# Half of one stream's convolution on ScalarE and VectorE instead of TensorE, in a selective-scan kernel

## The chip, the cores and the metric

One Trainium2 chip; the kernel runs on one of its cores. The metric is the device time of one execution in microseconds (us). TensorE (PE) multiplies matrices, with PEld for its weight loads; VectorE (DVE), ScalarE (ACT) and GpSimd (POOL) work element by element; SyncE (SP) issues DMAs.

## What is computed

For an input of 4 images, 128 channels, 96 x 96, the reference normalises in groups of 4 channels, reads each image as four sequences of 9216 positions (rows and columns, each forward and backward), runs the function below on each, fuses the four results and adds the input.

```python
def _scan1d(x, ...):
    t = _grouped1x1(x, in_proj_w, in_proj_b, G)          # 4 groups of 32 -> 128 channels
    u, gate = (t[:, :HID], t[:, HID:])                   # HID = 256
    u = jax.nn.silu(u)
    u = lax.conv_general_dilated(u, dw_w, ..., feature_group_count=HID)   # 5 taps a channel
    s = _conv1x1(u, ssm_in_w)                            # 32 channels
    a = DMIN + (DMAX - DMIN) * jax.nn.sigmoid(_conv1x1(u, ssm_delta_w, ssm_delta_b))
    a = jnp.clip(a, 0.0001, 0.9999)
    bb = jnp.tanh(_conv1x1(u, ssm_b_w, ssm_b_b))
    cc = jnp.tanh(_conv1x1(u, ssm_c_w, ssm_c_b))
    prefix = jnp.cumsum(jnp.log(a), axis=-1)
    hst = jnp.exp(prefix) * jnp.cumsum(bb * s * jnp.exp(-prefix), axis=-1)   # h = a*h + bb*s
    u = u + _conv1x1(cc * hst + ssm_d[None, :, None] * s, ssm_out_w)
    u = _grouped1x1(u * jax.nn.sigmoid(gate), mix_w, mix_b, G)
    return _conv1x1(u, out_proj_w, out_proj_b)
```

## The kernel before

Everything is float32. The host lays each sequence out in four phases (position modulo R = 4), so that a tile of 384 columns holds every fourth position of 1536. A phase of the program is one image in one orientation (V for columns, H for rows); it runs two streams s = 0 and 1, the forward and the backward sequence, in six steps of 1536 positions. A step has 8 units: four position phases p times two streams, k = 2p + s. So there are 8 x 6 x 8 = 384 units, and even units belong to stream 0, odd units to stream 1.

The work of a unit t is written out by hand, and each engine runs it in that order (a manual schedule):

- `products` (odd t, for the pair t-3): VectorE multiplies tanh(b) with s out of the PSUM tile pp (L410) and scales s by d (L411) into t1.
- `rows`: TensorE does the in-projection of unit t+8 (pf, L330) and, for the unit bi = t - LAG, the gate's projection (pg) and the recurrence's output projection pz, which reads the buffer t1. ScalarE takes tanh of pg (gv, L348); VectorE adds u to pz (L352) and multiplies by the gate (L353); ScalarE takes silu of pf (sil, L357).
- `conv` for j = 0 and 1, the two halves of 128 channels: eight matmuls each with banded 128 x 32 weights into pc, four 32-column tiles at a time; ScalarE copies pc to u (L375).
- `scan` (unit k = 1, for the step before): one recurrence instruction of 64 x 1536 (L418) over the buffer t0, which starts from the last element of the step before. `outputs` (odd t): c*h (L424), plus d*s (L425), copied to the other partitions by POOL (L426).
- statistics of the next image in even V units (`stats_chunk`), and once an image, in one unit, `stats_finish`: an alternation of small matmuls, VectorE and ScalarE instructions.
- `accumulate` (unit bi-1): the fused output projection py, added into the image-sized buffer acc (L443, L448, L450); in H phases finished rows are stored from acc and the next image's rows are loaded into it.
- `proj`: b, c, delta and s into pp for the pair of units; in odd units the half whose tanh goes to t0 (L396, then two POOL instructions), in even units the half whose tanh goes to t1 (L402).

PSUM: five banks rotate under one tag "x" (pf, pg, pc, py and small ones), one bank is pp's, two are pz's. t0 and t1 have two buffers each, so a step's buffers pass to the step after next. All matmuls go through one helper, line 300. Before the loop the kernel prepares banded weights on POOL and fuses the output weights: products on TensorE, copied out by VectorE (L274, L281), then pb (L286).

Of the kernel before, what the change touches and what calls it, by code (L numbers as in the profile page):

```python
# [30 lines left out]
P = 128  # L34
# [7 lines left out]
R = 4  # L42
# [1 line left out]
NS = HH // LN  # L44
N = LN * WW // R
M = WW // R
LAG = 11
UB = 8


# [1 line left out]
def conv_preact_kernel(  # L52
# [4 lines left out]
    in_wT: bass.AP,  # L57
    in_b: bass.AP,
    dw_v: bass.AP,
    proj_wT: bass.AP,  # L60
    proj_b: bass.AP,
    ssm_d: bass.AP,
# [47 lines left out]
    def psx(name):  # L110
        return ps.tile([P, 512], F32, tag="x", bufs=5, name=name)
# [37 lines left out]
        return stats[b]  # L149

    def stats_finish(b):
        mv = sp.tile([P, 2], F32, tag="mv", name=f"mv_{b}")
        nc.vector.bn_aggr(mv, stats[b].rearrange("p c s -> p (c s)"))
# [7 lines left out]
        nc.vector.scalar_tensor_tensor(ex, dev, dev, mv[:, 1:2], ALU.mult, ALU.add)  # L161
        pv = psx(f"pv_{b}")
# [6 lines left out]
        gm4 = sp.tile([P, 4], F32, tag="gm4", name=f"gm4_{b}")  # L169
        nc.vector.tensor_scalar_mul(gm4, gmask, norm[:, 0:1])  # L170
        pb = psx(f"pbn_{b}")
        nc.tensor.matmul(pb[:, 0:4], wn, gm4, start=True, stop=True)
# [49 lines left out]
    b_in = load(in_b, [P, 4], "b_in")  # L222
    w_proj = load(proj_wT, [P, 2, 4 * MH], "w_proj")
    b_proj = load(proj_b, [P, 2], "b_proj")
    d_sb = load(ssm_d, [P, 1], "d_sb")
# [10 lines left out]
    with tc.tile_pool(name="prep", bufs=1) as pp:  # L236
# [31 lines left out]
        for d in range(4):  # L268
            for j in range(2):
                pt = psx(f"pof_{d}_{j}")  # L270
                nc.tensor.matmul(
                    pt[:, :P], w_out[:, bass.ts(j, P)], w_fuse[:, d, :], start=True, stop=True
                )
                nc.vector.tensor_copy(w_of[:, d, j, :], pt[:, :P])  # L274
        for d in range(4):
            for j in range(2):
                pt = psx(f"pfin_{d}_{j}")
                nc.tensor.matmul(
                    pt[:, :P], w_mix[:, j, :], w_of[:, d, j, :], start=True, stop=True
                )  # L280
                nc.vector.tensor_scalar_mul(w_fin[:, d, j, :], pt[:, :P], 0.5)  # L281
# [16 lines left out]
    def mm(o, col, lhsT, rhs, start, stop):  # L298
        r = slice(32 * col, 32 * col + 32)
        nc.tensor.matmul(o[r, : rhs.shape[-1]], lhsT, rhs, start=start, stop=stop,  # L300
                         skip_group_check=True)


    sils = {}

    def rows(i, bi):

        front = gate = None
        if i is not None:
            step, k = divmod(i, UB)  # L310
            s, g = divmod(k, 4)
            un = units[step * UB + s]
            wn, _, bsil = stats[un["b"]]
# [41 lines left out]
        if front:  # L355
            for j in range(2):
                nc.scalar.activation(  # L357
                    sil[:, j, g, :], pf[j][:, : N + 1], AF.Silu, bias=bsil[:, j, g : g + 1]
                )
            if g == 3:  # L360
                if un["st"] == 0:
                    nc.gpsimd.memset(sil[0:64, :, :, 0:1], 0.0)
                if un["st"] == NS - 1:
                    nc.gpsimd.memset(sil[64:P, :, :, N : N + 1], 0.0)
                load_front(step + 1, s)

    def conv(un, j):
        sil = sils[un["step"], un["s"]]
        if j == 0:
            un["u"] = wk.tile([P, 2, N], F32, tag="u", bufs=LAG + 1, name=f"u_{un['id']}")  # L370
# [4 lines left out]
        nc.scalar.copy(un["u"][:, j, :], pc[:, :N])  # L375

    scans = {}
    qb, qc, qa, qs = (slice(MH * i, MH * (i + 1)) for i in range(4))
# [28 lines left out]
    def products(i):  # L407
        un = units[i]
        (ta, tb), p, pp = scans[un["step"]], un["p"], un["pp"]
        nc.vector.tensor_mul(ta[0:64, p, :], pp[64:P, :N], ta[0:64, p, :])  # L410
        nc.vector.tensor_scalar_mul(tb[64:P, p, :], pp[64:P, :N], d_sb[64:P, :])  # L411

    def scan(step):
        ta = scans[step][0]
        seq = ta.rearrange("p r n -> p (n r)")
        first = units[step * UB]["st"] == 0
        init = 0.0 if first else scans[step - 1][0][0:64, R - 1, N - 1 : N]
        nc.vector.tensor_tensor_scan(  # L418
            seq[0:64], seq[64:P], seq[0:64], init, ALU.mult, ALU.add
        )  # L420

    def outputs(step, p):
# [32 lines left out]
                nc.sync.dma_start(accf[:, r], xr[b + 1, :, r])  # L455


    def unit(t):
        bi = t - LAG
        if t >= 3 and t % 2 and t - 3 < NU:  # L460
            products(t - 3)
        rows(t + UB if t + UB < NU else None, bi if 0 <= bi < NU else None)
        if t < NU:
            conv(units[t], 0)
            conv(units[t], 1)
        if t >= UB + 1 and t % 2 and t - UB - 1 < NU:
            d = units[t - UB - 1]
            if d["p"] == 0:
                scan(d["step"])
            outputs(d["step"], d["p"])  # L470
        if t < NU:
            un = units[t]
            if un["order"] == "V" and t % 2 == 0 and un["b"] + 1 < B:
                stats_chunk(un["b"] + 1, (un["st"] * UB + un["k"]) // 2)
                if un["st"] == NS - 1 and un["k"] == UB - 2:
                    stats_finish(un["b"] + 1)
        if 0 <= bi - 1 < NU:
            accumulate(units[bi - 1])
        if t % 2 and t < NU:
            proj(t - 1, 0)  # L480
        elif t % 2 == 0 and 2 <= t <= NU:
            proj(t - 2, 1)

    stats_finish(b0)
    for i in range(UB):
        rows(i, None)
    with tc.manual_schedule(
        engines={nc.tensor.engine, nc.vector.engine, nc.scalar.engine, nc.gpsimd.engine}
    ):
        for t in range(NU + LAG + 1):  # L490
            unit(t)


_NAMES = [
    "xr", "xs", "in_wT", "in_b", "dw_v", "proj_wT", "proj_b", "ssm_d", "ssm_out_wT",
    "mix_w", "mix_b", "out_w", "out_b", "fuse_wT", "fuse_b",
]

# [61 lines left out]
```

## Time and profile before

| | |
|---|---|
| median of 3 runs | 2842.68 us (2841.59 to 2844.6) |
| the profiled execution | 2841.97 us |
| its span, first to last instruction | 2840.3 us |
| granted TensorE clock, mean | 0.996 of full speed |
| PE / PEld busy | 2749.8 / 1051.9 us |
| DVE / ACT / POOL busy | 1727.9 / 1436.3 / 499.6 us |
| DMA over the span | 134.55 MB, mean 47 GB/s |

A row of a group reads: line, engine, operation, output<-inputs by the program's names, shapes, count | busy us, mean ns of one | idle us of the engine just before them and what ended it. A row of the timeline reads: start in us, length in us, engine, line, operation; in brackets the idle time before it and its releaser. A row of waits reads: who waited <- for whom: us in total, times, longest. TensorE's rows overlap, since four or more small tiles run at once, and float32 matmuls have two records each.

### The profile page before, as it was taken

How to read it: one execution, taken by the hardware profiler on the slowest of the kernel's cores; microseconds unless marked ns; L12 is line 12 of the kernel's file. 1: busy time of each engine (PE TensorE's matmuls, PEld its weight loads, DVE VectorE, ACT ScalarE, POOL GpSimd, SP SyncE). 2: the span in 40 equal slices, each digit the busy share in tenths (PEclk: the TensorE clock that was granted, in tenths of full speed). 3: DMA queues.
4: the chain of work that ended last, by engine and by line, in shares of the span. 5: the costliest groups of instructions: out<-in, count | busy, mean ns of one | idle time of the engine just before them, and what ended most of it. 6: DMA issues, size and time to landing. Idle time of an engine off the chain costs nothing.

```text
span 2840.3 us, 95016 instructions
## 1 busy us (share of the span) xinstructions
PE 2749.8 (97%) x43088; PEld 1051.9 (37%) x43088; DVE 1727.9 (61%) x2119; ACT 1436.3 (51%) x2703; POOL 499.6 (18%) x754
## 2 busy tenths in 40 slices
PE   7999999999999999999999999999999999999998
PEld 3333333333333333333333333333333333333332
DVE  3466655655666666655666666655565656555667
ACT  3555555455555555555555555555555555555542
POOL 4111111111111111111111111111111111111110
PEclk9999999999999999999999999999999999999999
DMA  4111111112321111111232111111123111111111
GB/s 132 43 38 46 41 32 29 25 33 71 91 85 47 39 44 27 33 27 32 76 95 80 41 47 28 33 27 33 27 82 110 26 33 27 33 27 33 27 38 54
DMA packets 79156, 134.55 MB, mean 47 GB/s; under 512 B 11296, under 2 KB 73248, under 8 KB 78752
## 3 DMA queue, kind: packets, MB, share of 16 engines
q1 hardware_dynamic: 76704, 127.64, 16.6%
q8 instruction: 339, 5.55, 0.8%
q10 hardware_dynamic: 2048, 0.83, 0.1%
q14 instruction: 65, 0.53, 0.1%
HBM read 109.55 MB, written 18.87 MB: 45 GB/s over the span
## 4 chain that ended last, share of the span: by engine, by line
PE 82%; DVE 14%; issue 2%; ACT 1%; DMA 1%; SPq 0%; DVEq 0%
PE pc L300 32%; PE pp L300 16%; PE py L300 15%; PE pz L300 9%; PE pf L300 8%; DVE t L418 6%; DVE pz L352 2%; DVE gv L353 2%; PE pg L300 2%; DVE t L424 1%; DVE t L411 1%; ACT t L402 1%; DVE t L425 1%; DVE acc L443 1%; DVE acc L450 0%
## 5 line engine op out<-in xcount | busy, mean ns | idle before, releaser
L300 PE MATMUL pc<-sil,band 128*32 128x384 f32 x12288 | 1072.3, 489 | 50.2 <-DVE acc L443 27.1
L300 PEld LDWEIGHTS pc<-sil,band 128*32 128x32 f32 x12288 | 361.4, 109 | 738.3 <-issue 620.7
L352 DVE TENSOR_TENSOR pz<-pz,u 128x768 f32<-128x768 f32 x384 | 370.5, 965 | 346.4 <-PE pz L300 340.5
L375 ACT COPY u<-pc 128x384 f32<-128x384 f32 x768 | 367.6, 479 | 419.7 <-PE pc L300 415.5
L300 PE MATMUL pp<-u,w_proj 128*32 128x384 f32 x6144 | 571.4, 489 | 0.0
L300 PE MATMUL py<-gv,w_fin 128*32 128x384 f32 x6144 | 570.5, 489 | 0.7 <-DVE gv L353 0.7
L348 ACT ACTIVATE gv<-pg,bnorm 128x384 f32<-128x384 f32 x768 | 403.7, 578 | 101.3 <-PE pg L300 101.3
L300 PE MATMUL pz<-t,w_so 32*32 32x384 f32 x6144 | 430.3, 491 | 6.8 <-DVE gv L353 6.7
L396 ACT ACTIVATE t<-pp,b_proj 128x384 f32<-128x384 f32 x192 | 202.8, 1056 | 424.5 <-PE pp L300 314.5
L357 ACT ACTIVATE sil<-pf,bsilu 128x385 f32<-128x385 f32 x768 | 406.4, 590 | 3.3 <-PE pf L300 3.0
L426 POOL COPY t<-t 64x384 f32<-64x384 f32 x192 | 96.0, 500 | 1754.5 <-DVE t L425 1754.5
L353 DVE SCALAR_TENSOR_TENSOR gv<-gv,pz 128x768 f32<-128x768 f32 x384 | 366.5, 954 | 41.3 <-ACT u L375 0.9
L300 PE MATMUL pf<-x_in,wn 32*32 32x385 f32 x6144 | 356.7, 503 | 0.0
L300 PE MATMUL pg<-x_in,wn 32*32 32x384 f32 x6144 | 356.3, 494 | 0.0
L410 DVE TENSOR_TENSOR t<-pp,t 64x384 f32<-64x384 f32 x192 | 169.9, 885 | 298.8 <-ACT t L402 298.7
L402 ACT ACTIVATE t<-pp,b_proj 64x384 f32<-64x384 f32 x192 | 110.6, 576 | 409.0 <-PE pp L300 409.0
L300 PEld LDWEIGHTS pp<-u,w_proj 128*32 128x32 f32 x6144 | 204.5, 110 | 295.5 <-issue 267.3
L300 PEld LDWEIGHTS py<-gv,w_fin 128*32 128x32 f32 x6144 | 200.8, 110 | 298.2 <-issue 223.7
L399 POOL TENSOR_SCALAR t<-t 64x384 f32<-64x384 f32 x192 | 181.7, 946 | 317.4 <-ACT t L396 313.6
L300 PEld LDWEIGHTS pz<-t,w_so 32*32 32x32 f32 x6144 | 168.6, 103 | 163.1 <-issue 93.1
L443 DVE TENSOR_TENSOR acc<-py,acc 128x384 f32<-128x384 f32 x192 | 107.0, 557 | 194.0 <-PE py L300 176.4
L400 POOL TENSOR_SCALAR t<-t 64x384 f32<-64x384 f32 x192 | 182.6, 951 | 15.9
(60 smaller groups left out, 1006.3 us busy)
## 6 DMA issues: line engine op xcount, KB each, us to landing
x_in<-in_xs SPq DMA_DIRECT2D x96, 385.0 KB, 4.3
x_in<-in_xs SPq DMA_DIRECT2D x384, 96.2 KB, 2.4
out<-acc SPq DMA_DIRECT2D x24, 768.0 KB, 4.0
xs<-in_xr SPq DMA_DIRECT2D x72, 192.0 KB, 2.3
acc<-in_xr SPq DMA_DIRECT2D x18, 768.0 KB, 4.8
acc<-in_xr SPq DMA_DIRECT2D x24, 192.0 KB, 3.8
w_fuse<-in_fuse_wT ACTq DMA_DIRECT2D x1, 256.0 KB, 3.8
w_proj<-in_proj_wT ACTq DMA_DIRECT2D x1, 128.0 KB, 4.5
```

The lines of the kernel that those rows point to most:

```text
L300: nc.tensor.matmul(o[r, : rhs.shape[-1]], lhsT, rhs, start=start, stop=stop, skip_group_check=True)
L348: nc.scalar.activation(gv[:, j, :], pg[j][:, :N], AF.Tanh, bias=gbn[:, 2 + j : 3 + j], scale=0.5)
L352: nc.vector.tensor_add(pz[:, :, :N], pz[:, :, :N], bu["u"])
L353: nc.vector.scalar_tensor_tensor(gv, gv, 1.0, pz[:, :, :N], ALU.add, ALU.mult)
L357: nc.scalar.activation(sil[:, j, g, :], pf[j][:, : N + 1], AF.Silu, bias=bsil[:, j, g : g + 1])
L375: nc.scalar.copy(un["u"][:, j, :], pc[:, :N])
L396: nc.scalar.activation(ta[:, p, :], pp[:, :N], AF.Tanh, bias=b_proj[:, 0:1])
L399: nc.gpsimd.tensor_scalar(a, a, half, DMIN + half, ALU.mult, ALU.add)
L400: nc.gpsimd.tensor_scalar(a, a, 0.9999, 0.0001, ALU.min, ALU.max)
L402: nc.scalar.activation(tb[0:64, p, :], pp[0:64, :N], AF.Tanh, bias=b_proj[0:64, 1:2])
L410: nc.vector.tensor_mul(ta[0:64, p, :], pp[64:P, :N], ta[0:64, p, :])
L418: nc.vector.tensor_tensor_scan(seq[0:64], seq[64:P], seq[0:64], init, ALU.mult, ALU.add)
```

## The change

Stream 0's second half of channels (j = 1, even units) is no longer convolved on TensorE. Its silu tile is laid out with all 128 channels on the partitions for each position phase; one ScalarE instruction scales it by tap 0 into a PSUM bank, in the unit before (`taps(un, [0])`), and four VectorE instructions add taps 1 to 4 in place, the last one into u, at the start of the unit. A tap's weight is a per-partition scalar from a new small input, w_tap. d*s moves from VectorE to ScalarE (`skip`). The recurrence is two instructions of 768 positions, in the units k = 1 and 2, after the accumulate. `outputs` come two units later, and LAG is 12. `stats_finish` is a generator that advances by one part a unit. The copies of the fused weights are ScalarE's.

```diff
-LAG = 11
+LAG = 12
@@ stats_finish
         nc.vector.bn_aggr(mv, stats[b].rearrange("p c s -> p (c s)"))
+        yield
...
-                nc.vector.tensor_copy(w_of[:, d, j, :], pt[:, :P])
+                nc.scalar.copy(w_of[:, d, j, :], pt[:, :P])
...
-                nc.vector.tensor_scalar_mul(w_fin[:, d, j, :], pt[:, :P], 0.5)
+                nc.scalar.mul(w_fin[:, d, j, :], pt[:, :P], 0.5)
@@ rows
-                    mm(pf[j], c, wn[r, 32 * g : 32 * g + 32], x_in[s][r, c, :], True, True)
+                    m, q = (c, g) if by_taps(s, j) else (g, c)
+                    mm(pf[j], c, wn[r, 32 * m : 32 * m + 32], x_in[s][r, q, :], True, True)
@@ new
+    def by_taps(s, j):
+        return s == 0 and j == 1
+    def taps(un, ks):
+        sil, j = sils[un["step"], un["s"]], 1
+        if 0 in ks:
+            un["pt"] = psx(f"pt_{un['id']}")
+        for k in ks:
+            off, q = divmod(un["p"] + k, R)
+            src, part = sil[:, j, q, off : off + N], un["pt"][:, :N]
+            if k == 0:
+                nc.scalar.activation(part, src, AF.Copy, scale=w_tap[:, 0:1])
+            else:
+                nc.vector.scalar_tensor_tensor(
+                    un["u"][:, j, :] if k == K - 1 else part,
+                    src, w_tap[:, k : k + 1], part, ALU.mult, ALU.add)
@@ products, skip, scan
-        nc.vector.tensor_scalar_mul(tb[64:P, p, :], pp[64:P, :N], d_sb[64:P, :])
+    def skip(i):
+        nc.scalar.activation(
+            tb[64:P, un["p"], :], un["pp"][64:P, :N], AF.Copy, scale=d_sb[64:P, :])
+    def scan(step, part):
+        r = bass.ts(part, R * N // 2)
+        if part:
+            init = ta[0:64, R - 1, N // 2 - 1 : N // 2]
@@ unit, new order
+        bi, k = t - LAG, t % UB
+        if t % 2 and 0 <= t - 3 < NU:
             products(t - 3)
+        if t % 2 and 0 <= t - 11 < NU:
+            outputs(d["step"], d["p"])          # d = units[t - 11]
+        if un and k % 2 == 0:
+            taps(un, range(1, K))
         rows(t + UB if t + UB < NU else None, bi if 0 <= bi < NU else None)
+        if t % 2 and 0 <= t - 3 < NU:
+            skip(t - 3)
+        if un:
+            conv(un, 0)
+            if k % 2:
+                conv(un, 1)
         if 0 <= bi - 1 < NU:
             accumulate(units[bi - 1])
+        if later:
+            next(later[0], None)
...                                             # statistics chunk
+        if k in (1, 2) and 0 <= t // UB - 1 < NU // UB:
+            scan(t // UB - 1, k - 1)
+        if t + 1 < NU:
+            new_u(units[t + 1])
+            if k % 2:
+                taps(units[t + 1], [0])
...                                             # proj as before
```

More of the change, by code (lines that the diff above doesn't have):

```diff
@@ L59, in conv_preact_kernel @@
     dw_v: bass.AP,
+    dw_c: bass.AP,
     proj_wT: bass.AP,
@@ L161, in stats_finish @@
         nc.vector.scalar_tensor_tensor(ex, dev, dev, mv[:, 1:2], ALU.mult, ALU.add)
+        gm4 = sp.tile([P, 4], F32, tag="gm4", name=f"gm4_{b}")
+        nc.vector.tensor_scalar_mul(gm4, gmask, norm[:, 0:1])
+        yield
         pv = psx(f"pv_{b}")
@@ L222, in conv_preact_kernel @@
     b_in = load(in_b, [P, 4], "b_in")
+    w_tap = load(dw_c, [P, K], "w_tap")
     w_proj = load(proj_wT, [P, 2, 4 * MH], "w_proj")
@@ L357, in rows @@
                 nc.scalar.activation(
-                    sil[:, j, g, :], pf[j][:, : N + 1], AF.Silu, bias=bsil[:, j, g : g + 1]
+                    sil[:, j, g, :],
+                    pf[j][:, : N + 1],
+                    AF.Silu,
+                    bias=bn[:, j : j + 1] if by_taps(s, j) else bsil[:, j, g : g + 1],
                 )
             if g == 3:
[L361 to L364, printed above, removed]
+                for j in range(2):
+                    if un["st"] == 0:
+                        r = (slice(0, P), slice(0, 2)) if by_taps(s, j) else (slice(0, 64), slice(0, 4))
+                        nc.gpsimd.memset(sil[r[0], j, r[1], 0:1], 0.0)
+                    if un["st"] == NS - 1:
+                        r = (slice(0, P), slice(2, 4)) if by_taps(s, j) else (slice(64, P), slice(0, 4))
+                        nc.gpsimd.memset(sil[r[0], j, r[1], N : N + 1], 0.0)
                 load_front(step + 1, s)
@@ L375, in conv, with new_u @@
         nc.scalar.copy(un["u"][:, j, :], pc[:, :N])
+    def new_u(un):
+        un["u"] = wk.tile([P, 2, N], F32, tag="u", bufs=LAG + 1, name=f"u_{un['id']}")
+    def taps(un, ks):
[10 more added lines that the diff above has]
+                    un["u"][:, j, :] if k == K - 1 else part,
+                    src,
+                    w_tap[:, k : k + 1],
+                    part,
+                    ALU.mult,
+                    ALU.add,
+                )
     scans = {}
@@ L410, in products @@
         nc.vector.tensor_mul(ta[0:64, p, :], pp[64:P, :N], ta[0:64, p, :])
-        nc.vector.tensor_scalar_mul(tb[64:P, p, :], pp[64:P, :N], d_sb[64:P, :])
-    def scan(step):
+    def skip(i):
+        un = units[i]
+        tb = scans[un["step"]][1]
+        nc.scalar.activation(
+            tb[64:P, un["p"], :], un["pp"][64:P, :N], AF.Copy, scale=d_sb[64:P, :]
+        )
+    def scan(step, part):
         ta = scans[step][0]
         seq = ta.rearrange("p r n -> p (n r)")
-        first = units[step * UB]["st"] == 0
-        init = 0.0 if first else scans[step - 1][0][0:64, R - 1, N - 1 : N]
+        r = bass.ts(part, R * N // 2)
+        if part:
+            init = ta[0:64, R - 1, N // 2 - 1 : N // 2]
+        elif units[step * UB]["st"] == 0:
+            init = 0.0
+        else:
+            init = scans[step - 1][0][0:64, R - 1, N - 1 : N]
         nc.vector.tensor_tensor_scan(
-            seq[0:64], seq[64:P], seq[0:64], init, ALU.mult, ALU.add
+            seq[0:64, r], seq[64:P, r], seq[0:64, r], init, ALU.mult, ALU.add
         )
@@ L455, in accumulate @@
                 nc.sync.dma_start(accf[:, r], xr[b + 1, :, r])
+    later = []
     def unit(t):
-        bi = t - LAG
-        if t >= 3 and t % 2 and t - 3 < NU:
+        bi, k = t - LAG, t % UB
+        un = units[t] if t < NU else None
+        if t % 2 and 0 <= t - 3 < NU:
             products(t - 3)
-        rows(t + UB if t + UB < NU else None, bi if 0 <= bi < NU else None)
[L463 to L476, printed above, removed]
+        if t % 2 and 0 <= t - 11 < NU:
+            d = units[t - 11]
+            outputs(d["step"], d["p"])
+        if un and k % 2 == 0:
+            taps(un, range(1, K))
+        rows(t + UB if t + UB < NU else None, bi if 0 <= bi < NU else None)
+        if t % 2 and 0 <= t - 3 < NU:
[4 more added lines that the diff above has]
+                conv(un, 1)
         if 0 <= bi - 1 < NU:
             accumulate(units[bi - 1])
-        if t % 2 and t < NU:
+        if later:
+            next(later[0], None)
+        if un and un["order"] == "V" and k % 2 == 0 and un["b"] + 1 < B:
+            stats_chunk(un["b"] + 1, (un["st"] * UB + k) // 2)
+            if un["st"] == NS - 1 and k == UB - 2:
+                later[:] = [stats_finish(un["b"] + 1)]
+        if k in (1, 2) and 0 <= t // UB - 1 < NU // UB:
[4 more added lines that the diff above has]
+                taps(units[t + 1], [0])
+        if k % 2 and un:
             proj(t - 1, 0)
-        elif t % 2 == 0 and 2 <= t <= NU:
+        elif k % 2 == 0 and 2 <= t <= NU:
             proj(t - 2, 1)
-    stats_finish(b0)
+    for _ in stats_finish(b0):
+        pass
     for i in range(UB):
         rows(i, None)
+    new_u(units[0])
+    taps(units[0], [0])
     with tc.manual_schedule(
@@ L525 @@
         .reshape(P, 2, 4, 8),
+        "dw_c": v["dw_w"].reshape(HID, K)[P:],
         "proj_wT": halves(
```

9 lines of the change are left out of this document (3 added, 6 removed).

## The prediction, made before the changed kernel was run

> **What bounds the kernel now.** I read the page first: the shares of the engines and the chain that ended last.
>
> ```profile
> PE 2749.8 (97%) x43088; PEld 1051.9 (37%) x43088; DVE 1727.9 (61%) x2119; ACT 1436.3 (51%) x2703; POOL 499.6 (18%) x754
> PE 82%; DVE 14%; issue 2%; ACT 1%; DMA 1%; SPq 0%; DVEq 0%
> PE pc L300 32%; PE pp L300 16%; PE py L300 15%; PE pz L300 9%; PE pf L300 8%; DVE t L418 6%; DVE pz L352 2%; DVE gv L353 2%; PE pg L300 2%; DVE t L424 1%; DVE t L411 1%; ACT t L402 1%; DVE t L425 1%; DVE acc L443 1%; DVE acc L450 0%
> ```
>
> TensorE (PE) works without a break and the convolution (pc) is the largest part of the chain. The timeline shows two consecutive units of the middle, an odd one with the recurrence and the even one behind it:
>
> ```profile
> 999.63 1.47 PE L300 MATMUL py<-gv,w_fin 128*32 128x384 f32 x16
> 1001.17 0.56 DVE L443 TENSOR_TENSOR acc<-py,acc 128x384 f32<-128x384 f32 x1 [0.18 <-PE py L300]
> 1002.32 0.51 PE L300 MATMUL pf<-x_in,wn 32*32 32x385 f32 x2
> ...
> 1010.01 1.12 PE L300 MATMUL pz<-t,w_so 32*32 32x384 f32 x16
> 1011.06 2.79 PE L300 MATMUL pc<-sil,band 128*32 128x384 f32 x32
> 1013.67 1.47 PE L300 MATMUL py<-gv,w_fin 128*32 128x384 f32 x16
> 1013.72 3.41 DVE L418 TENSOR_TENSOR_SCAN t<-t,t 64x1536 f32<-64x1536 f32 x1
> 1014.96 1.48 PE L300 MATMUL pp<-u,w_proj 128*32 128x384 f32 x16
> 1016.36 0.51 PE L300 MATMUL pf<-x_in,wn 32*32 32x385 f32 x2
> 1017.04 1.11 PE L300 MATMUL pz<-t,w_so 32*32 32x384 f32 x16
> 1017.16 0.89 DVE L424 TENSOR_TENSOR t<-t,t 64x384 f32<-64x384 f32 x1
> 1017.22 0.97 ACT L396 ACTIVATE t<-pp,b_proj 128x384 f32<-128x384 f32 x1 [2.83 <-DVE t L418]
> 1018.08 0.56 DVE L425 TENSOR_TENSOR t<-t 64x384 f32<-64x384 f32 x1
> 1018.67 0.56 DVE L443 TENSOR_TENSOR acc<-py,acc 128x384 f32<-128x384 f32 x1
> 1019.28 2.79 PE L300 MATMUL pc<-sil,band 128*32 128x384 f32 x32 [1.13 <-DVE acc L443]
> ```
>
> Counting from a unit's first pf: pz at 0.68, pc at 1.72 (1011.06 is 1.05 behind pz), py 2.61 after pc, the next unit at 7.02 (1002.32 + 2 x 7.02 = 1016.36). The accumulate of the last py ends at 1001.73, 0.59 before the next pf. Once a step (8 units) the recurrence holds the accumulate back, and pc waits 1.13 for the bank that it frees:
>
> ```profile
> L300 PE MATMUL pc<-sil,band 128*32 128x384 f32 x12288 | 1072.3, 489 | 50.2 <-DVE acc L443 27.1 <-DVE acc L450 23.0
> ACT t L396 <- DVE t L418: 109.9, 39, 3.0
> ```
>
> 50.2 us in all are these waits. So the bank that pc takes is the accumulate's, freed just ahead of the rows' own. The second row: the first tanh of a step waits for the recurrence, which only reads one element of the buffer that the tanh takes over. A buffer is passed on only when all that read its old content are done.
>
> **The change, part by part.** Prices:
>
> ```profile
> L353 DVE SCALAR_TENSOR_TENSOR gv<-gv,pz 128x768 f32<-128x768 f32 x384 | 366.5, 954 | 41.3 <-ACT u L375 0.9 <-DVE pz L352 0.9
> L352 DVE TENSOR_TENSOR pz<-pz,u 128x768 f32<-128x768 f32 x384 | 370.5, 965 | 346.4 <-PE pz L300 340.5
> L375 ACT COPY u<-pc 128x384 f32<-128x384 f32 x768 | 367.6, 479 | 419.7 <-PE pc L300 415.5 <-ACT sil L357 0.2
> L396 ACT ACTIVATE t<-pp,b_proj 128x384 f32<-128x384 f32 x192 | 202.8, 1056 | 424.5 <-PE pp L300 314.5 <-DVE t L418 109.9
> L402 ACT ACTIVATE t<-pp,b_proj 64x384 f32<-64x384 f32 x192 | 110.6, 576 | 409.0 <-PE pp L300 409.0
> L410 DVE TENSOR_TENSOR t<-pp,t 64x384 f32<-64x384 f32 x192 | 169.9, 885 | 298.8 <-ACT t L402 298.7
> L418 DVE TENSOR_TENSOR_SCAN t<-t,t 64x1536 f32<-64x1536 f32 x40 | 136.4, 3409 | 1.3
> L411 DVE TENSOR_SCALAR t<-pp,d_sb 64x384 f32<-64x384 f32 x192 | 119.8, 624 | 2.8
> L443 DVE TENSOR_TENSOR acc<-py,acc 128x384 f32<-128x384 f32 x192 | 107.0, 557 | 194.0 <-PE py L300 176.4 <-PE pg L300 8.2 <-PE pz L300 4.7
> L448 DVE SCALAR_TENSOR_TENSOR acc<-py,b_fin,acc 128x384 f32<-128x384 f32 x96 | 59.3, 618 | 179.1 <-PE py L300 179.1
> ```
>
> (1) TensorE loses pc for j=1 in every even unit: two of four rounds, 2.61/2 = 1.305 us, 192 times: -250.6. An even unit becomes 5.71, a pair 12.73.
>
> (2) In its place ScalarE writes tap 0 into a PSUM bank (nearest L402, 0.58, without the 0.479 copy of L375) and VectorE adds four taps. A tap is L448's form (pointer scalar, one PSUM input), 0.618; PSUM as output adds L352 less L353, 0.01. Four with three gaps of 0.03 (as between L424 and L425 in the timeline): T = 2.59. VectorE's sum: 1727.9 + 768 x 0.624 - 119.8 (L411, moved to ScalarE, 0.58 each) + 10 (two halves of the recurrence at 1.81 for one of 3.41: 3.2 of it is elements, 0.2 fixed, my split) = 2097. ScalarE: 1436 + 192 x (0.58 + 0.58 - 0.48) = 1567. Neither is the bound by its sum; it is the order that costs.
>
> (3) The tap bank. The taps are VectorE's first work in an even unit and free their bank ahead of the rows', so pc takes it, as it took the accumulate's. An ordinary pair: accumulate done at -0.59, taps from -0.56 to 2.03, pc at 2.08 instead of 1.72: 0.36 of wait, a new one in units 0, 4 and 6 of each step. [...]
>
> (4) The recurrence. Its first half stands in unit 1 behind the accumulate, and so ahead of the taps of unit 2: taps done at 3.87, pc at 3.92, wait 2.20. Should pc take the first gate bank instead: the tanh L396 waits for that half (to 1.25), then 1.06, then the first gv (L402's kind, 0.58): pc at 2.9, wait 1.2. No row decides between them; I take the middle, 1.70. The second half (1.84 with its gap) stands behind the accumulate of unit 2 and reaches 1.3 to 1.9 into unit 3.
>
> (5) LAG 12. The last pz that reads a step's buffer t1 moves from unit 2 to unit 3, while the tanh L402 that takes this buffer over stays at the end of unit 2. By the L396 row it waits for all readers: until pz of unit 3 is done (0.68 + 1.11), to 2.41 with its own 0.58, not 0.71. The products (L410) start at 2.44; products 0.92, outputs 1.50, pz and gv 2.01, accumulate 0.56, no gap left: about 7.4, 0.35 to 0.43 into unit 4 instead of 0.59 ahead of it. Taps to 2.97, pc at 3.02: wait 1.30 in unit 4 in place of 0.36. The products wait behind that tanh, and skip (ScalarE) behind the products, but skip's slot, near 4.6, is long before pp of unit 3.
>
> Sum of waits in a step: 0.36 + 1.70 + 1.30 + 0.36 = 3.72; 46.5 full steps: +173. The old 50.2 go. In the first 12 units there is no gate work: tap 0 comes at the end of the odd unit as before, but pc sooner, by pz's 1.05 at least: T has less cover, an estimated 1.6 more in five pairs, +8.
>
> (6) Statistics over units:
>
> ```profile
> 1046.32 1.11 PE L300 MATMUL pz<-t,w_so 32*32 32x384 f32 x16
> 1053.55 0.36 PE L172 MATMUL pbn<-gm,wn 128*128 128x4 f32 x2 [1.10 <-DVE gm L170]
> 1058.92 1.12 PE L300 MATMUL pz<-t,w_so 32*32 32x384 f32 x16
> ```
>
> 12.60 instead of 7.02, three times; three small matmuls of 0.36 stay each time: -(5.58 - 1.1) x 3 = -13.4. The rest hides in units with waits.
>
> (7) Weight copies on ScalarE:
>
> ```profile
> 24.71 2.31 DVE L281 TENSOR_SCALAR w_fin<-pfin 128x128 f32<-128x128 f32 x8
> 29.75 1.84 PE L286 MATMUL pb<-b_out,w_fuse 128*128 128x1 f32 x8
> 31.71 0.79 DVE L153 BATCH_NORM_AGGREGATE mv<-bn 128x2 f32<-128x144 f32 x1
> ```
>
> The statistics' matmul queues behind pb, and pb behind copies that wait among VectorE's bn_stats. ScalarE is free there; at best the 4.7 between 27.0 and 31.7 go, at worst nothing: -4.
>
> (8) Image change, three times. The first V accumulate waits for the store and reload of acc:
>
> ```profile
> 801.08 0.56 DVE L450 TENSOR_TENSOR acc<-py,acc 128x384 f32<-128x384 f32 x1
> 801.66 0.35 SPq L453 DMA_DIRECT2D out<-acc  x1
> 805.87 0.33 SPq L455 DMA_DIRECT2D acc<-in_xr  x1
> 810.39 0.56 DVE L443 TENSOR_TENSOR acc<-py,acc 128x384 f32<-128x384 f32 x1 [3.84 <-PE pg L300]
> ```
>
> 8.7 us pass. The shift by a unit makes the two accumulates 6.5 apart, and taps stand behind: +2 each, +6. SP's order of loads and stores is otherwise the same. LAG's extra unit at the end costs VectorE's 0.97 + 0.95 + 0.56 and half of L424 and L425, 3.2, less 2.3 of gate work (pz 1.05, py 1.29) that leaves the loop: +0.9. The more and smaller memsets on POOL (18% busy) and the load of w_tap lie beside other work: nothing; without cover some 0.1 each.
>
> Sum: -250.6 - 50.2 + 173 + 8 - 13.4 - 4 + 6 + 0.9 = -130.3, from the profiled execution's 2841.97 (span 2840.3; 0.7 under the median of the runs, 2842.68): **2712 us**.
>
> **Rivals.** (A) No late tanh: the buffer is passed on by parts, since the slices differ. The L396 row speaks against it. 0.94 x 46.5 less: 2668. (B) pc takes a bank other than the taps', in all pairs (a gate bank, free at about pc's turn in ordinary pairs). Left are 1.2 in unit 2 and 0.4 in unit 4 (the rows' own wait for the late accumulate), 74 for 173, and the 8 fall away: 2605. For it: nothing says the pool must keep its order with a new tenant. (C) Cheap taps, at L443's 0.557 and without gaps: T 2.23, the two waits of 0.36 go and the others lose as much, about 1.2 a step: 2656. L448's 0.618 for the very form speaks against it. [...] (D) Dear taps, which makes it slower: every 0.1 us on a tap adds 0.4 to all four waits of a step, 75 us in all; from 0.80 a tap the gain is gone. L410 pays 0.885 for 384 elements beside PSUM, on strided data; at that price, 0.26 more than mine, it would be 2712 + 195 = 2907. The taps read contiguous rows, so little speaks for it. (E) The freed TensorE time comes back nearly whole in waits of several kinds, within 0.2%.
>
> **How the numbers follow.** Forecast 0.37, A 0.18, B 0.20, C 0.08, D 0.08, E 0.04; 0.05 for A and B or C together, under 2595. Range 2595 to 2775: its low end takes in B, its high end a tap chain with gaps of 0.09 and the 2.20 of point 4 (2712 + 33 + 23, and some for the bounds of 5 and 7). Unlisted waits can push toward slower. About 0.2% is what a measurement of this kernel can tell from no change: faster 0.88, same 0.03, slower 0.09.
>
> **What would show it.** pc with 9216 records; a group of 768 VectorE taps near 0.62 us; pc's idle row naming the taps with some 0.4 in ordinary pairs and 1 to 2 in unit 2; L402's successor waiting for a pz in unit 3 once a step; VectorE near 78%; no 5.6 us hole at the statistics. It is wrong if pc's idle falls to some tens of us (B), if taps take 0.8 (D), or if TensorE waits elsewhere, on sil or gv.

## The result, and the profile after

The changed kernel takes 2751.27 us (median of 4 runs, 2736.34 to 2756.05) against 2843.07 us for the kernel before in the same session: a ratio of 0.9667, interval [0.9636, 0.9699], 92 us less. The profiled execution is the one of 2736.34 us, with a span of 2734.7 us. The page's rows of the engines and of the chain:

```profile
PE 2546.5 (93%) x40016; PEld 961.4 (35%) x40016; DVE 2054.6 (75%) x2727; ACT 1565.1 (57%) x2912; POOL 496.1 (18%) x786
PE 64%; DVE 30%; ACT 2%; DMA 2%; issue 1%; ACTq 0%; DVEq 0%; SPq 0%
PE pc L308 25%; PE py L308 16%; DVE pt L406 12%; PE pp L308 10%; PE pz L308 6%; PE pf L308 6%; DVE u L406 4%; DVE t L468 3%; DVE gv L365 2%; DVE acc L498 2%; DVE pz L364 2%; DVE acc L493 2%; DVE t L448 1%; DVE t L474 1%; PE pg L308 1%
```

TensorE is no longer busy without a break (93% of the span, 97% before), and the taps (L406), absent before, are 16% of the chain. The groups, with shapes kept apart:

```profile
L308 PE MATMUL pc<-sil,band 128*32 128x384 f32 x9216 | 833.3, 494 | 153.2 <-DVE u L406 145.9 <-ACT gv L360 7.3
L406 DVE SCALAR_TENSOR_TENSOR pt<-sil,w_tap,pt 128x384 f32<-128x384 f32 x576 | 357.3, 620 | 43.6 <-ACT pt L404 28.5
L406 DVE SCALAR_TENSOR_TENSOR u<-sil,w_tap,pt 128x384 f32<-128x384 f32 x192 | 118.1, 615 | 6.8
```

The convolution has lost 239 us of busy time (1072.3 before) and 3072 records; 153.2 us of idle time stand ahead of it in place of 50.2, nearly all ended by the last tap. The waits of the tanh that fills the recurrence's second tile:

```profile
ACT t L440 <- PE pp L308: 300.6, 146, 2.6
ACT t L440 <- PE pz L308: 194.9, 46, 5.5
```

46 times, once a step, it waits for pz instead of for its own input. The timeline of units 0, 1 and 2 of one step:

```profile
617.60 1.48 PE L308 MATMUL pp<-u,w_proj 128*32 128x384 f32 x16
618.39 1.93 DVE L406 SCALAR_TENSOR_TENSOR pt<-sil,w_tap,pt 128x384 f32<-128x384 f32 x3
619.68 1.12 PE L308 MATMUL pz<-t,w_so 32*32 32x384 f32 x16
620.35 0.61 DVE L406 SCALAR_TENSOR_TENSOR u<-sil,w_tap,pt 128x384 f32<-128x384 f32 x1
621.02 1.50 PE L308 MATMUL pc<-sil,band 128*32 128x384 f32 x16 [0.23 <-DVE u L406]
...
626.75 2.79 PE L308 MATMUL pc<-sil,band 128*32 128x384 f32 x32
...
631.55 1.81 DVE L468 TENSOR_TENSOR_SCAN t<-t,t 64x768 f32<-64x768 f32 x1
632.72 1.12 PE L308 MATMUL pz<-t,w_so 32*32 32x384 f32 x16
633.39 1.94 DVE L406 SCALAR_TENSOR_TENSOR pt<-sil,w_tap,pt 128x384 f32<-128x384 f32 x3
635.36 0.61 DVE L406 SCALAR_TENSOR_TENSOR u<-sil,w_tap,pt 128x384 f32<-128x384 f32 x1
636.03 1.72 PE L308 MATMUL pc<-sil,band 128*32 128x384 f32 x16 [2.19 <-DVE u L406]
637.50 2.81 PE L308 MATMUL py<-gv,w_fin 128*32 128x384 f32 x16
```

In unit 0 pc starts 1.34 us after pz, and 0.05 us after the last tap has ended. In unit 1, which has no taps, it starts 1.04 after pz; in unit 2 half a recurrence (L468) runs before the taps and pc starts 3.31 after pz. Right behind that gap py takes 2.81 us, not the 1.47 that it took before. The same place in windows of 2 us (the third number from the end of a row is the granted TensorE clock):

```profile
634.00:636.00 2.00, 0.00 (x0) 0.00 (x0) 1.89 (x5) 2.00 (x5) 1.45 (x2) 1.00 0.24 58
636.00:638.00 2.00, 1.97 (x20) 0.77 (x24) 1.81 (x2) 0.35 (x2) 0.34 (x1) 0.80 0.00 0
638.00:640.00 2.00, 2.00 (x16) 0.65 (x12) 0.00 (x0) 0.28 (x1) 0.00 (x0) 0.50 0.00 0
640.00:642.00 2.00, 2.00 (x36) 0.73 (x44) 1.61 (x2) 0.00 (x0) 0.00 (x0) 0.85 0.00 0
```

The clocks read 1.00, 0.80, 0.50 and 0.85. A window of 2 us loses 2 us times what its clock lacks: 0.4 + 1.0 + 0.3 = 1.7 us, as much as 3.4 us at half clock would lose. A step (8 units) is best read from the same pc of consecutive steps (here the first four records of unit 0), in the timelines of before and of after:

```profile
545.41 0.53 PE L300 MATMUL pc<-sil,band 128*32 128x384 f32 x4
602.74 0.53 PE L300 MATMUL pc<-sil,band 128*32 128x384 f32 x4
```

```profile
399.38 0.53 PE L308 MATMUL pc<-sil,band 128*32 128x384 f32 x4 [0.17 <-DVE u L406]
455.94 0.53 PE L308 MATMUL pc<-sil,band 128*32 128x384 f32 x4 [0.23 <-DVE u L406]
...
510.96 0.53 PE L308 MATMUL pc<-sil,band 128*32 128x384 f32 x4 [0.23 <-DVE u L406]
565.99 0.53 PE L308 MATMUL pc<-sil,band 128*32 128x384 f32 x4 [0.23 <-DVE u L406]
```

57.33 us before; 55.03 after in a step whose clock stays up, 56.56 in one with a half-clock stretch.

### The profile page after: what moved, and what is told of

It reads as the page before. It is cut to its first block, busy times and chain, and to the rows that moved or that the text cites. A ratio compares the mean times of both kernels' runs of the same rounds, so it can differ in the third digit from the quotient of the medians.

```text
span 2734.7 us, 89086 instructions
## 1 busy us (share of the span) xinstructions
PE 2546.5 (93%) x40016; PEld 961.4 (35%) x40016; DVE 2054.6 (75%) x2727; ACT 1565.1 (57%) x2912; POOL 496.1 (18%) x786
## 3 DMA queue, kind: packets, MB, share of 16 engines
q1 hardware_dynamic: 76704, 127.64, 17.5%
## 4 chain that ended last, share of the span: by engine, by line
PE 64%; DVE 30%; ACT 2%; DMA 2%; issue 1%; ACTq 0%; DVEq 0%; SPq 0%
PE pc L308 25%; PE py L308 16%; DVE pt L406 12%; PE pp L308 10%; PE pz L308 6%; PE pf L308 6%; DVE u L406 4%; DVE t L468 3%; DVE gv L365 2%; DVE acc L498 2%; DVE pz L364 2%; DVE acc L493 2%; DVE t L448 1%; DVE t L474 1%; PE pg L308 1%
## 5 line engine op out<-in xcount | busy, mean ns | idle before, releaser
L308 PE MATMUL pc<-sil,band 128*32 128x384 f32 x9216 | 833.3, 494 | 153.2 <-DVE u L406 145.9
L308 PE MATMUL py<-gv,w_fin 128*32 128x384 f32 x6144 | 584.5, 499 | 0.7 <-DVE gv L365 0.7
L308 PEld LDWEIGHTS pc<-sil,band 128*32 128x32 f32 x9216 | 258.7, 109 | 709.2 <-issue 272.2
L308 PE MATMUL pz<-t,w_so 32*32 32x384 f32 x6144 | 445.9, 492 | 4.6 <-DVE gv L365 4.5
L391 ACT COPY u<-pc 128x384 f32<-128x384 f32 x576 | 271.6, 480 | 231.8 <-PE pc L308 227.0
L440 ACT ACTIVATE t<-pp,b_proj 64x384 f32<-64x384 f32 x192 | 110.7, 577 | 495.5 <-PE pp L308 300.6
L406 DVE SCALAR_TENSOR_TENSOR pt<-sil,w_tap,pt 128x384 f32<-128x384 f32 x576 | 357.3, 620 | 43.6 <-ACT pt L404 28.5
L308 PE MATMUL pg<-x_in,wn 32*32 32x384 f32 x6144 | 375.6, 494 | 4.2 <-DVE acc L493 4.2
L308 PE MATMUL pf<-x_in,wn 32*32 32x385 f32 x6144 | 375.9, 503 | 0.0
L434 ACT ACTIVATE t<-pp,b_proj 128x384 f32<-128x384 f32 x192 | 198.8, 1036 | 285.4 <-PE pp L308 187.1
L448 DVE TENSOR_TENSOR t<-pp,t 64x384 f32<-64x384 f32 x192 | 171.4, 893 | 221.4 <-ACT t L440 221.4
L437 POOL TENSOR_SCALAR t<-t 64x384 f32<-64x384 f32 x192 | 174.3, 908 | 876.1 <-ACT t L434 876.1
L369 ACT ACTIVATE sil<-pf,bsilu 128x385 f32<-128x385 f32 x576 | 314.9, 586 | 3.2 <-PE pf L308 3.0
```

The lines of the kernel that those rows point to most:

```text
L369: nc.scalar.activation(sil[:, j, g, :], pf[j][:, : N + 1], AF.Silu, bias=bn[:, j : j + 1] if by_taps(s, j) else bsil[:, j, g : g + 1],)
L406: nc.vector.scalar_tensor_tensor(un["u"][:, j, :] if k == K - 1 else part, src, w_tap[:, k : k + 1], part, ALU.mult, ALU.add,)
L434: nc.scalar.activation(ta[:, p, :], pp[:, :N], AF.Tanh, bias=b_proj[:, 0:1])
L437: nc.gpsimd.tensor_scalar(a, a, half, DMIN + half, ALU.mult, ALU.add)
L440: nc.scalar.activation(tb[0:64, p, :], pp[0:64, :N], AF.Tanh, bias=b_proj[0:64, 1:2])
```

## The experiments

Theory: the time that left TensorE is real, and what came back is three waits, each with its own cause (the bank that the taps hold, the half recurrence ahead of the taps of unit 2, the tanh held up by its buffer), and the half clock after the longest of them. The rivals were that pc would be as late in another bank, that the taps are late by themselves, and that the buffer doesn't matter.

**Where the taps' sum lies.** With a bank of its own (so four rotate):

```diff
-        return ps.tile([P, 512], F32, tag="x", bufs=5, name=name)
+        return ps.tile([P, 512], F32, tag="x", bufs=4, name=name)
-            un["pt"] = psx(f"pt_{un['id']}")
+            un["pt"] = ps.tile([P, 512], F32, tag="t", name=f"pt_{un['id']}")
```

> The tap sum gets a PSUM bank of its own and the rotating pool has four banks instead of five. Theory (the wait is for the bank that the taps free): pc in even units takes a gate bank that is free in time; the idle time ahead of pc falls from 153 us to about 60, what is left being some 1.2 in unit 2 (the tanh that waits for the recurrence holds the gate's own tanh) and under 1 in unit 4; with no gap of 2 us TensorE's clock keeps 1.0 in the loop; 2625 to 2670 us against 2751. Rival (VectorE is simply too late in even units, whatever the bank, or four banks are too few): the wait moves to the accumulate's bank or to the rows, and the time stays at 2735 to 2760 or rises.

2655.08 us, ratio to the kernel before 0.9344 [0.933, 0.9358]: the time is as expected, though pc's idle time fell to 94 us and not to 60. pc's group, then units 2 and 3 with the tanh (ACT) that stands ahead of the gate's own:

```profile
L308 PE MATMUL pc<-sil,band 128*32 128x384 f32 x9216 | 830.9, 493 | 94.3 <-ACT gv L360 93.6
```

```profile
622.21 0.94 ACT L434 ACTIVATE t<-pp,b_proj 128x384 f32<-128x384 f32 x1 [2.76 <-DVE t L468]
623.54 1.50 PE L308 MATMUL pc<-sil,band 128*32 128x384 f32 x16 [0.94 <-ACT gv L360]
...
629.44 0.57 ACT L440 ACTIVATE t<-pp,b_proj 64x384 f32<-64x384 f32 x1 [3.85 <-PE pz L308]
630.53 2.79 PE L308 MATMUL pc<-sil,band 128*32 128x384 f32 x32 [1.19 <-ACT gv L360]
```

No wait names the taps any more. What is left are gate banks, freed late by ScalarE: in unit 2 its tanh (L434) waits for the half recurrence, in unit 3 the other tanh (L440) waits for pz.

With the sum in SBUF and five rotating banks kept:

```diff
-            un["pt"] = psx(f"pt_{un['id']}")
+            un["pt"] = wk.tile([P, N], F32, tag="pt", bufs=1, name=f"pt_{un['id']}")
```

> The changed kernel with one edit: the taps' sum lies in an SBUF tile, not in one of the five rotating PSUM banks. Theory (what costs 2.2 us in unit 2 and 0.3 us in units 0, 4 and 6 is the bank that the taps hold, not that they are late as such): the convolution finds a free bank, its idle time behind the taps goes, the late tanh stays; 2640 to 2670 us as with a bank of its own. Rival (taps are slower in SBUF, 0.7 us or more each, so that VectorE becomes the bound): 2720 to 2850 us, with TensorE waiting for VectorE's accumulate in every even unit.

2572.98 us, 0.9047 [0.9033, 0.9061]: better than either expected, although the taps became dearer, as the rival said. The instructions of the taps' line (min/median/max ns), with the sum in a bank of its own and then in SBUF:

```profile
L406 DVE SCALAR_TENSOR_TENSOR u<-sil,w_tap,pt x192: 614/615/617, 40.5 to 2592.4; 128x384 f32<-128x384 f32 x192
```

```profile
L406 DVE SCALAR_TENSOR_TENSOR u<-sil,w_tap,pt x192: 617/1176/1410, 40.9 to 2507.8; 128x384 f32<-128x384 f32 x192
```

and the last tap of units 2 and 4 in the second, with GpSimd's work:

```profile
602.72 1.14 POOL L438 TENSOR_SCALAR t<-t 64x384 f32<-64x384 f32 x1
603.07 1.20 DVE L406 SCALAR_TENSOR_TENSOR u<-sil,w_tap,pt 128x384 f32<-128x384 f32 x1
...
614.84 1.14 POOL L438 TENSOR_SCALAR t<-t 64x384 f32<-64x384 f32 x1
616.42 0.62 DVE L406 SCALAR_TENSOR_TENSOR u<-sil,w_tap,pt 128x384 f32<-128x384 f32 x1
```

Beside this GpSimd instruction the last tap takes 1.20, without one 0.62. Of the run's 768 taps 269 take over 0.7 us, and each of them overlaps a GpSimd instruction; the 385 that overlap none take 0.62 at most. (The other 114 overlap one too and are no slower.) The kernel is still faster: VectorE, 86% busy, has room, and pc, 11.2 us idle in all, stands behind a late bank only in three places, with the accumulate.

Is it the fifth rotating bank, then? The sum in SBUF again, but with `bufs=4` for tag "x", so that one bank is left empty:

> The changed kernel with the taps' sum in SBUF and four rotating PSUM banks in place of five (one bank is left empty). Theory (the 80 us by which the sum in SBUF beat a bank of its own is the fifth rotating bank: with four, the convolution and gate banks come late in units 2 and 3): 2645 to 2680 us, TensorE waiting in front of the convolution for ScalarE's gate as with the bank of its own. Rival (the 80 us come from the sum's place itself, though a tap costs more there): within 10 us of the sum in SBUF with five banks, 2565 to 2585 us.

2701.72 us, 0.9506 [0.9492, 0.952]. Taking away the one bank costs 129 us, so the rival falls. It is also 47 us more than with a bank of its own, where four banks rotate too, and pc's idle time behind ScalarE is the same in both (93.9 and 93.6 us). The difference lies ahead of pc, in unit 3:

```profile
582.14 0.55 DVE L500 TENSOR_TENSOR acc<-py,acc 128x384 f32<-128x384 f32 x1
582.74 0.10 PEld L308 LDWEIGHTS pg<-x_in,wn 32*32 32x32 f32 x1 [0.70 <-DVE acc L500]
585.67 2.79 PE L308 MATMUL pc<-sil,band 128*32 128x384 f32 x32 [1.19 <-ACT gv L360]
```

VectorE, behind the dearer taps of unit 2, does the accumulate late, and pg waits for the bank that it frees: from the unit's first pf to the last pg 1.26 us pass instead of 0.46, some 38 us over the run. So the dear taps do cost where banks are short.

**The late tanh.** Three buffers for the tile that it fills:

```diff
-                wk.tile([P, R, N], F32, tag="t1", name=f"t1_{step}"),
+                wk.tile([P, R, N], F32, tag="t1", bufs=3, name=f"t1_{step}"),
```

> The buffer t1 exists three times instead of twice, nothing else. Theory (a buffer is passed on only when all its readers are done, so the tanh of unit 2 waits for pz of unit 3): the 195 us of that tanh's waits for pz vanish, products start some 1.7 us earlier in unit 3, pc's wait in unit 4 falls from about 1.2 to 0.3; about 40 us less, 2700 to 2720. Rival (unit 4 is late because the second half of the recurrence reaches into unit 3): the waits for pz vanish but unit 4 stays late, 2740 to 2755.

2708.41 us, 0.9523 [0.9503, 0.9543]: 43 us from one buffer. The waits now:

```profile
ACT t L440 <- PE pp L308: 407.2, 192, 3.5
```

All 192 wait for their input, none for pz. Unit 4 starts pc 1.34 after pz (median), like units 0 and 6; unit 2 stays at 3.31.

Both edits together, with three buffers for t0 as well:

> Own bank for the tap sum, and t0 and t1 three times each. Theory: besides what the two changes alone give, the tanh of unit 1 no longer waits for the recurrence, so the gate bank is free in time in unit 2 too; left is VectorE's lateness after two recurrence halves in a row, under 1 us in unit 4; no half clock in the loop: 2550 to 2600. Rival (TensorE cannot use its freed time since VectorE with its 2055 us of work and fixed order is the real bound): above 2640, with new waits for the accumulate or gv.

2580.9 us, 0.9084 [0.9071, 0.9098]: the time is as expected. pc's idle time is 2.5 us in all (in unit 3 the rows ahead of it still take 0.5 longer, since pg waits for the accumulate's bank):

```profile
L308 PE MATMUL pc<-sil,band 128*32 128x384 f32 x9216 | 829.8, 492 | 2.5 <-ACT gv L360 1.5
```

The three buffers added to the sum in SBUF:

> The changed kernel with the taps' sum in SBUF, five rotating PSUM banks, and three buffers for each of the recurrence's two tiles. Theory (the late tanh still holds ScalarE back once a step; what TensorE still waits, 40 us over the whole run, is partly VectorE late behind it): the wait of ScalarE's tanh for the gate's products goes, 2535 to 2565 us. Rival (five free banks already cover the late tanh, and what is left is VectorE, slowed by taps that share SBUF with GpSimd): the same within 6 us, 2567 to 2580 us.

2572.71 us, 0.9054 [0.904, 0.9067]; without them it was 0.9047 [0.9033, 0.9061]. The tanh's wait for pz (170.4 us and 46 times with two buffers) is gone, yet the time stays: the rival was right, five free banks cover the late tanh.

**The recurrence and the taps.** The whole recurrence in unit 1, as before the change, but the rest changed:

```diff
-        r = bass.ts(part, R * N // 2)
+        r = slice(0, R * N)
-        if k in (1, 2) and 0 <= t // UB - 1 < NU // UB:
+        if k == 1 and 0 <= t // UB - 1 < NU // UB:
```

> The recurrence in one instruction again, at the place of its first half. Theory: taps of unit 2 start 1.6 us later (3.41 for 1.81), pc's wait there grows from 2.2 to 3.8, 74 us; the longer gap lets TensorE's clock fall to half more often than in 18 of 48 steps, up to 50 us more: 2825 to 2880, and a mean clock under 0.975. Rival (the clock has nothing to do with the gap): the clock stays at 0.98 and the time at 2820 to 2830.

2790.79 us, 0.9821 [0.9785, 0.9857]: slower by 40 us than in halves, less than either expected. pc waited 2.6 in unit 2, not 3.8, for it then stood behind another bank, and not at all in the second step of each phase. From pz to pc the waits add up to 187 us over the run, as with halves (185); what got worse is the clock (78.4 us lost in the loop for 29.0, counted as in the last section):

```profile
L308 PE MATMUL pc<-sil,band 128*32 128x384 f32 x9216 | 852.5, 503 | 154.9 <-ACT gv L360 100.0 <-DVE u L406 54.9
```

Which half delays which unit? With three buffers for both tiles (`bufs=3` for t0 and t1, not shown), the halves after units 1 and 3:

```diff
-LAG = 12
+LAG = 14
-        if t % 2 and 0 <= t - 11 < NU:
-            d = units[t - 11]
+        if t % 2 and 0 <= t - 13 < NU:
+            d = units[t - 13]
-        if k in (1, 2) and 0 <= t // UB - 1 < NU // UB:
-            scan(t // UB - 1, k - 1)
+        if k in (1, 3) and 0 <= t // UB - 1 < NU // UB:
+            scan(t // UB - 1, k // 2)
```

> The version with three buffers for the recurrence's tiles (2708 us; taps still in a rotating bank), with the recurrence's halves in units 1 and 3 rather than 1 and 2 and the outputs two units later. Theory (prediction's step 4: the 2.2 us in unit 2 come from the half of the recurrence that stands ahead of that unit's taps on VectorE, and the half clock follows that gap): the wait of unit 2 falls to the 0.3 us of the other even units, 47 times 1.9 us and some 20 halvings at 1.7 us less, 2585 to 2625 us. Rival (the taps of unit 2 are late whatever runs ahead of them, or the half in unit 3 delays an accumulate as much): 2660 to 2720 us.

2858.58 us, 1.0056 [1.0039, 1.0073]: slower than before the change. The expectation had the place wrong. `scan` stands at the end of a unit, so a half in an odd unit is ahead of the next even unit's taps, and this run has two such places a step, where the changed kernel has one (its second half, in unit 2, precedes unit 3, which has no taps). It doubled the suspected cost:

```profile
603.63 1.50 PE L308 MATMUL pc<-sil,band 128*32 128x384 f32 x16 [2.19 <-DVE u L406]
618.64 2.53 PE L308 MATMUL pc<-sil,band 128*32 128x384 f32 x16 [2.19 <-DVE u L406]
...
633.38 1.50 PE L308 MATMUL pc<-sil,band 128*32 128x384 f32 x16 [0.22 <-DVE u L406]
646.42 1.50 PE L308 MATMUL pc<-sil,band 128*32 128x384 f32 x16 [0.23 <-DVE u L406]
```

Against the version with three buffers for t1 it is 150 us more: from pz to pc 81 us more over the run (227 for 146), and 68 more lost to the clock in the loop (105.5 for 37.4).

The converse, halves after units 2 and 4 (`k in (2, 4)`, `k // 2 - 1`), so that no taps follow either:

> As the version with the recurrence's halves after units 1 and 3 (2859 us, two waits of 2.2 us a step), but with the halves after units 2 and 4, so that each stands ahead of an odd unit, in which VectorE has no taps. Theory (prediction's step 4, the half ahead of the taps is the wait): every even unit waits only the 0.3 us of the others; against the version with three buffers (2708 us, one such wait a step) 47 times 1.9 us and most of its 53 us of lost clock fall away, 2560 to 2610 us, with a clock of 0.99. Rival (a half after unit 4 makes the accumulate of unit 5 late, as the halves after units 1 and 3 did with a bank of its own): 2620 to 2700 us.

2598.12 us, 0.9135 [0.912, 0.9151]: from the same edits as the run above, and 260 us apart from it by the place of two instructions. The rival falls. pc's group:

```profile
L308 PE MATMUL pc<-sil,band 128*32 128x384 f32 x9216 | 827.8, 491 | 44.8 <-DVE u L406 44.8
```

Only the 0.3 of each even unit is left, and the clock is 0.997.

The halves after units 1 and 3 on the version with a bank of its own and three buffers (the diff of LAG above):

> The own-bank, three-buffer version with the recurrence's halves in units 1 and 3 rather than 1 and 2, and the outputs two units later. Theory (the 0.5 us that TensorE still waits in unit 3 of each step comes from VectorE being behind after two halves of 1.8 us in a row): up to 20 us less, 2557 to 2575 us. Rival (each half now delays an accumulate by itself, in units 3 and 5, and the fill grows by two units): the same or more, 2580 to 2605 us.

2603.57 us, 0.9158 [0.9144, 0.9171]: 23 us slower than without it, the rival's case. pc comes 0.5 us late in two units a step where there was one (pz to pc 1.6 us for 1.05 to 1.12), since pg waits for the accumulate's bank, 20 us over the run; the two more units at the end take 6.

**Statistics and start**, both on that version. Finishing the statistics in one unit (`for _ in stats_finish(...): pass`):

> The own-bank, three-buffer version with the finishing of the batch statistics back in one unit. Theory (the prediction's statistics term: a hole of 5.6 us at each of the three finishes that the trace of before shows, of which spread finishing leaves about 1.1, and the half clock that followed each hole there): three times 4.5 us, about 13 us more, 2590 to 2600 us, with a hole of 4 to 6 us on TensorE at each finish. Rival (the finish lies beside TensorE's work now that two of four convolution rounds have left it): the same time within 4 us, 2577 to 2585 us.

2601.58 us, 0.9149 [0.9136, 0.9163], 21 us more, just above the theory. The small matmuls of one finish, in this run and in the spread version:

```profile
325.06 0.35 PE L160 MATMUL pm<-mv,gmean 128*128 128x1 f32 x2 [2.08 <-DVE mv L157]
326.20 0.56 PE L171 MATMUL pv<-ex,gmean 128*128 128x1 f32 x2 [0.79 <-DVE gm L168]
327.72 0.56 PE L179 MATMUL pbn<-gm,wn 128*128 128x4 f32 x2 [0.96 <-DVE wn L176]
```

```profile
334.32 0.38 PE L160 MATMUL pm<-mv,gmean 128*128 128x1 f32 x2
341.90 0.38 PE L171 MATMUL pv<-ex,gmean 128*128 128x1 f32 x2
348.65 0.39 PE L179 MATMUL pbn<-gm,wn 128*128 128x4 f32 x2
```

Spread, none of them makes TensorE wait. The first pc of this run also came 3.3 us later (48.36 for 45.02), so some 17.5 of the 21 are the three finishes, 5.8 each. Part of it is clock: behind the first and the third finish two half-clock stretches follow, behind the second one.

The copies of the weights on VectorE again (`nc.vector.tensor_copy`, `nc.vector.tensor_scalar_mul`):

> The own-bank, three-buffer version with the copies of the output weights back on VectorE. Theory (the prediction's copy term: unit 0's first convolution comes about 4 us earlier because VectorE is rid of the copies): 4 us more, about 2585 us, with the first convolution 4 us later. Rival (the start is bounded by the weights' transfers): no change, 2579 to 2583 us.

2586.79 us, 0.9096 [0.9081, 0.9111] against 0.9084 [0.9071, 0.9098]: the intervals overlap. In the traces the first pc comes at 50.77 instead of 45.02, 5.75 us later, which is what the medians differ by (5.9). But in the twelve traces with the copies on ScalarE it comes anywhere from 44.51 to 48.36, so this speaks for the theory without showing its size.

## Why the prediction came out where it did

The forecast was 2712 in a range of 2595 to 2775; the median is 2751 and the profiled execution, with which the sum is compared, 2736.

- **(1), (2) The trade.** pc's busy time fell by 239 against 250.6 predicted; part of the rest is half clock, for in the version with halves after units 2 and 4 (clock 0.997) it fell by 244.5. Taps at 0.620 and 0.615 (0.618 predicted) with gaps of 0.03, ScalarE 1565.1 (1567). VectorE 2054.6 (2097): its records overlap, by 65 us in all where it was 25 before, which the sum had not allowed for. Half a recurrence took 1.81 (1.81 put). Ordinary pairs had their wait, and L448's price was the right one. Rivals C and D fall.
- **(3) The tap bank**: as put. pc waits in units 0 and 6 for the last tap, 0.24 to 0.30 us (0.36 predicted). A bank of its own took the wait away, which shows the cause. Rival B, that pc takes a gate bank anyway, did not happen in the changed kernel; where it was enforced it gave 2655, not 2605, since the late tanh frees a gate bank late too.
- **(4) The half recurrence**: the mechanism was right, and its size was at the end of the range that the prediction set aside: 2.14 to 2.27 us, not the 1.70 that lay between 2.20 and 1.2. Halving the difference was the error: for the other even units the prediction had already let pc take the taps' bank, and unit 2 is no exception. The runs with the halves after units 1 and 3, and 2 and 4, show the step to be causal.
- **(5) The late tanh**: right as put, 1.15 to 1.19 in unit 4 (1.30 predicted). Three buffers took away 43 us where rival A had 44.
- **The sum of the waits**: pz to pc, less the 1.045 without a wait, comes to 185.5 us over the whole run for 173 predicted. The 8 us in the first 12 units did not come: pc didn't wait for taps there. A step of the prediction is 57.33 - 5.22 - 1.08 + 3.72 = 54.75; measured 54.78 in V phases and 55.03 in H phases, where the clock stays up. That it is so close is in part luck: unit 2 waited 0.5 longer than predicted, units 0, 4 and 6 0.2 to 0.4 less together.
- **What the prediction had no term for: the clock.** Of the 45 steps from unit 16 to unit 376, 18 are longer than 55.6, most of them 1.5 to 1.7 longer than the others (56.56 above), some at a change of phase or image. By windows of 2 us over the whole trace, 17 half-clock stretches of 1.7 lie in the loop, 29.0 us. Before had 5 (8.5 us), all at its three statistics finishes, and so in the 12.60 from which point (6) took its saving; the 29.0 are all on top. With +12.5 for the waits, -8 for the start, -5 for the old waits (55.5 by the distance of pz to pc, 50.2 by the row used), -4 for the statistics and +1.9 at the end (both below) this is 26; the miss is 24. The spread of the runs (2736 to 2756) goes with their clock, 0.983 to 0.976.
- **(6) to (8)**: the statistics brought more than 4.5 each: the steps with a finish were 5.6 to 7.0 longer than the others before and are 0.7 longer now (two of them with a half-clock stretch besides), so 17.6 in all (13.4 predicted; 17.5 in the run that finishes them in one unit). The first pc came 4.1 us sooner (44.68 for 48.82; -4 predicted), but the traces with the copies on ScalarE scatter over 3.9 us there, so the agreement can be luck. The time from the unit behind the last convolution to the end of the span grew by 2.8 (0.9 predicted). The three steps with an image change were 1.6 to 4.6 us longer than the others, of which a half clock may be 1.7: +2 each is not refuted.
- **Rival E** would have the freed time back whole: of the 300.8 us taken out by (1) and the old waits, 185 came back as waits and 29 as clock.

## What to carry to other kernels

Before work moves off the busiest engine, ask which rotating buffer the new work holds while it runs and who is next in line for it: here the place of the sum alone, with five banks left to the others, decided 178 us (2751 to 2573), although the taps' price rose with it. One more buffer was worth 43 us where a bank came late anyway, and nothing where five were free. A long instruction on the helping engine belongs behind work that somebody waits for, not ahead of it: two halves of a recurrence moved by one unit made 2859 us into 2598. With a median of 2572.7 to 2573.0 us (0.9047 and 0.9054), the sum in SBUF with five free banks is the best version here, though its taps cost up to 2.3 times as much.

## What the runs showed of the hardware

**TensorE's clock fell by half after idle gaps of 2.2 us.** Half-clock stretches of about 1.7 us lost each, counted in windows of 2 us from 60 us to the last unit's pc, by the longest waits that recur in each step:

| kernel | recurring waits ahead of pc, us a step | lost in the loop, us | mean clock |
|---|---|---|---|
| halves after units 2, 4 | 0.3, four times | 1.7 | 0.997 |
| sum in SBUF, five banks | none | 8.5 | 0.991 |
| own bank, three buffers | none (0.5 in the rows ahead) | 8.5 | 0.990 |
| before | 1.1 | 8.5 | 0.996 |
| taps in a bank of their own | 1.0 and 1.25 | 8.6 | 0.990 |
| sum in SBUF, four banks | 1.0 and 1.25 (and 0.8 in the rows ahead) | 13.7 | 0.989 |
| after | 2.2 and 1.2 | 29.0 | 0.983 |
| three buffers for t1 | 2.2 | 37.4 | 0.980 |
| recurrence whole | 2.6 and 1.2 | 78.4 | 0.971 |
| halves after units 1, 3 | 2.2, twice | 105.5 | 0.961 |

The mean clock has the start in it too: ahead of 60 us the same count gives up to 14 us in some of these and nothing in others (11.9 us after; none before, whose first clock record begins at 51.1 us). What that cost was not shown. Recurring waits of up to 1.25 us hardly cost clock: versions with none lose as much, at the changes of image. Of gaps of 2.2 between a third and two thirds did (after: 16 of 46, which measure 2.07 to 2.72 us), each for about 3.4 us. The clock records say which: in the traces of these ten kernels the clock changes only on a grid of 3.41 us that runs through the whole loop. In those of before and after together, of 1499 stretches of that grid at full clock with under 1.3 us of TensorE idle none was followed by half clock, of 18 with 2.05 us or more all were, and of the 23 between two. So a gap of 2.2 cost clock here when most of it fell into one stretch of the grid.

**VectorE and GpSimd.** With one SBUF and one PSUM input the last tap took 614 to 617 ns over 192 instructions, 187 of which overlap one of GpSimd's, in the run with a bank of its own, and 614 to 616 in the changed kernel, where 182 do. With two SBUF inputs it took 617 to 1410, the long ones all beside a GpSimd instruction. By what the two hold each other up was not shown. That the later of them waits for the whole of the other wasn't either: the tap of 603.07 above ends 0.41 us after GpSimd's instruction, less than the 0.62 that it takes alone.
